# Turning the attention probabilities of a perceiver block: VectorE in blocks over all rows, ScalarE moving the pieces to their keys' rows

## Chip, cores and metric

The kernel runs on one core of one Trainium2 chip, in float32 throughout. The metric is the device time of one execution in microseconds (us). The time before is 783.33 us, the median of three runs (782.91 to 785.45).

## What is computed

There are B = 16 samples of S = 128 tokens with D = 512 features, and each sample has V = 2048 context rows of 512 features. The block is, cut to what matters:

```python
x = x + cross_attention(layernorm(x), ctx)      # softmax(x ctx^T) ctx, one head, 2048 keys
x = x + self_attention(layernorm(x))            # 16 heads of 32, rotary on half of each head, causal, 128 keys
x = x + ffn(layernorm(x))                       # h + two of eight low-rank experts, chosen by token 0 of the sample
```

The change touches the self attention only. For each of its 16 heads it has a 128 x 128 matrix of probabilities, queries on the rows. The product with the values needs it turned, keys on the rows. The mask is causal: with queries and keys cut into four groups of 32, query group i needs key groups j = 0 to i only, so ten of the sixteen 32 x 32 blocks of a head hold anything.

## The kernel before

**Layout.** A tile has 128 rows (partitions). `att` holds the probabilities of one sample as 128 queries x 16 heads x 128 keys. `pT` is one constant tile, 128 keys x 4 query groups x 16 heads x 32 queries, set to zero once at the start, so the six blocks per head above the diagonal are zero for good and only the ten others are written for each sample.

**The loop.** The main loop (line 849) has 14 passes, b = 0 to 13. It works on several samples at a time: in pass b the self attention is that of sample b, the cross attention's second half (`attend`) is that of sample a = b + 1, the cross attention's first half (`score`) is that of sample s = b + 2, and the expert stage is that of sample l = b - 1. The last two samples are finished after the loop in an order of their own, and they turn their probabilities on TensorE (`turn_heads`), which the change leaves alone.

**What sets the order.** Every engine and SP's DMA queue run their instructions in the order in which the program issues them; the wrapper `InOrder` keeps the scheduler from moving any. Inside an engine's queue an instruction that waits holds up all that follow it. All work goes through that wrapper, so the profile gives line 101 for nearly everything, and tiles are told apart by name.

**The stretch of a pass that the change is in**, in program order, with the engine of each step:

- `attend(a, 3)`, TensorE: the last matmuls into the two PSUM banks `av`; `whole(a)`: TensorE turns the partial sums into `den`.
- `attended(a)`, ScalarE: copies `moved` and the first half of `first` out of `av`.
- `turn_probs(b, 0)`, VectorE.
- `begin_join(a)`: VectorE adds into `moved`, then into `av`; then ScalarE copies the second half of `first`.
- `turn_probs(b, 1)`, VectorE.
- `joined(a)`, `portion(a)`, `x1_of(a)`, VectorE: two more adds into `av`, the softmax's divisor `rden`, the residual stream, and the moments of the second norm (`st`, `mv`). The second add overwrites what the copy of the second half of `first` reads, so it waits for that copy. GpSimd makes `rs` and `sh` from `mv`.
- `score(s, 0)`, TensorE, into a PSUM bank `psc`; `keep_score(s, 0)`: ScalarE copies it to `sc`.
- `turn_probs(b, 2)`, VectorE; `pair(l)`, ScalarE: copies `each`, which two gathering DMAs brought, to `paired`; `rows(2, a)`, ScalarE: the normed rows `h`, from `sh` and `rs`.
- `score(s, 1)`, TensorE; `keep_score(s, 1)`: ScalarE copies to `sc`, then VectorE takes the running maximum `mx` out of the same bank.
- `turn(2, a)`: VectorE turns `h` in 32 x 32 blocks into a tile `turn`, and SP's queue sends it through DRAM (`d`) back to the tile `hT`.
- `turn_probs(b, 3)`, VectorE.
- `rows(1, s+1)` on ScalarE and `turn(1, s+1)` as above, for a later sample.
- `score(s, 2)`, TensorE; `middle(l)`: TensorE `mid`, from `paired`, and ScalarE takes it out of PSUM; `keep_score(s, 2)`; `score(s, 3)`; `heads(b)`: TensorE multiplies `pT` with the values into `y`; `widen(l)`: `ffn`; `keep_heads(b)`: ScalarE copies `y` to `yT`; `keep_score(s, 3)`; `join(b)`: TensorE `o`, from `yT`.

**Banks and tiles.** The pool for `psc` has two banks, so `score(s, 2)` needs the bank of `score(s, 0)` empty again, and `score(s, 3)` needs that of `score(s, 1)`, copied by ScalarE and read by VectorE's maximum. Two engines that read one bank do so one after the other: the maximum waits for the copy. The tag `turn` has two buffers, used in turn.

**Turning before.** `turn_probs(b, i)` (line 556) takes query group i. For each key group j up to i one VectorE transpose reads rows 32i to 32i + 31 of `att`, all 16 heads, and writes the turned blocks to rows 32j to 32j + 31 of `pT`: 1, 2, 3 and 4 instructions of 32 x 512 in the four calls.

Of the kernel before, what the change touches and what calls it, by code (L numbers as in the profile page):

```python
# [11 lines left out]
F32 = mybir.dt.float32  # L12
# [7 lines left out]
P = 128  # L20
# [3 lines left out]
Q = P // 32  # L24
# [42 lines left out]
def perceiver_block(ctx: ExitStack, tc: tile.TileContext, io: dict, out: bass.AP):  # L67
# [4 lines left out]
    p2 = ctx.enter_context(tc.tile_pool(name="p2", bufs=2))  # L72
# [17 lines left out]
    pT = const.tile([P, Q, H, 32], F32, name="pT")  # L90
# [12 lines left out]
    pe, dve, act, pool, sp = map(InOrder, (nc.tensor, nc.vector, nc.scalar, nc.gpsimd, nc.sync))  # L103
# [17 lines left out]
    class Norm:  # L121
# [24 lines left out]
        def rows(self):  # L146
            of = p2 if self.tag == "h" else p1
            self.h = of.tile([P, D], F32, tag=self.tag, name=f"{self.tag}_{self.name}")[: self.n]
            to, of = self.h, self.src
            if self.by_act:  # L150
                act.activation(to, of, AF.Identity, bias=self.shift, scale=self.rstd)
                return self
            if self.mixed:
                to = to.rearrange("p (c a j) -> p c a j", c=KC, j=Q)
                of = of.rearrange("p (c j a) -> p c a j", c=KC, j=Q)
            dve.tensor_scalar(to, of, self.mv[:, 0:1], self.rstd, ALU.subtract, ALU.mult)
            return self
# [70 lines left out]
    def load_x(b):  # L228
        if b < B:
            xs[b] = p3.tile([P, D], F32, tag="x", name=f"x_{b}")  # L230
            load(xs[b], io["x"][b])

    def load_turned(b, v):
        if b < B:
            t = p4.tile([P, KC, 512], F32, tag="ctxT", name=f"ctxT_{b}_{v}")
            load(t, io["ctxT"][b, v])
            turned_cts[b, v] = t
# [13 lines left out]
    atts, ys, yTs, os_, routes, mids, ffns = ({} for _ in range(7))  # L251
# [4 lines left out]
    def turn(n, b):  # L256
        hTs[n, b] = norms[n, b].turned()
# [15 lines left out]
    def keep_score(b, v):  # L273
        if v == 0:
            scs[b] = p1.tile([P, VC, 4, S], F32, tag="blocks" if b == 1 else "sc", name=f"sc_{b}")
            mxs[b] = p1.tile([P, 4, S], F32, tag="mx", name=f"mx_{b}")
        sc, mx, ps = scs[b], mxs[b], psc.pop((b, v))
        act.copy(sc[:, v], ps)
        if 0 < v < VC - 1:
            dve.tensor_tensor(mx, ps, mx if v > 1 else sc[:, 0], ALU.max)  # L280
        if v == VC - 1:
            most = p1.tile([P, S], F32, tag="most", name=f"most_{b}")
            for to, in0, in1 in (
                (mx[:, 2:], ps[:, 2:], mx[:, 2:]), (ps[:, :2], ps[:, :2], mx[:, :2]),
                (mx[:, 3], ps[:, 1], mx[:, 3]), (ps[:, 0], ps[:, 0], mx[:, 2]), (most, ps[:, 0], mx[:, 3]),
            ):
                dve.tensor_tensor(to, in0, in1, ALU.max)
            mxs[b] = most
# [5 lines left out]
    def turn_max(b):  # L294
        trs[b] = bank(ps_acc, "acc", f"tr_m_{b}")
        transpose(trs[b][:, :S], mxs.pop(b), ident)

    def most(b):
        nm = p2.tile([P, 1], F32, tag="nm", name=f"nm_{b}")
        dve.tensor_reduce(nm, trs.pop(b)[:, :S], AX.X, ALU.max, negate=True)  # L300
        trs[b] = nm

    def spread(b):
        spreads[b] = bank(ps_acc, "acc", f"spread_{b}")
        transpose(spreads[b][:, :S], trs.pop(b).to_broadcast([P, P]), ident)

    def less(b, v):
        sc = scs[b]
        dve.tensor_tensor(
            sc[:, v], sc[:, v], spreads[b][:, None, :S].to_broadcast([P, 4, S]), ALU.add  # L310
        )

    def power(b, v):
        act.activation(scs[b][:, v], scs[b][:, v], AF.Exp)
# [145 lines left out]
    def project(b, n, ms=range(HC)):  # L460
        hT = hTs[2, b]
        if 0 in ms:
            projected[n, b] = bank(ps_acc, "acc", f"{n}_{b}")
        ps = projected[n, b]
        for m in ms:
            for c in range(KC):
                matmul(
                    ps[:, m * P : (m + 1) * P], w[n][:, c, m * P : (m + 1) * P], hT[:, :, c, :],
                    start=(c == 0), stop=(c == KC - 1),
                )  # L470

    def rotate(b, n, by=pool):
        ps = projected.pop((n, b))
        partner = p1.tile([P, HC, S], F32, tag=f"{n}P", name=f"{n}P_{b}")
        dve.stream_shuffle(partner.rearrange("p c t -> p (c t)"), ps, PARTNERS)
        ps = ps.rearrange("p (c t) -> p c t", c=HC)
        dve.tensor_tensor(
            ps, ps, cst[:, None, C_COS : C_COS + S].to_broadcast([P, HC, S]), ALU.mult
        )
        by.tensor_tensor(  # L480
            partner, partner, cst[:, None, C_SIN : C_SIN + S].to_broadcast([P, HC, S]), ALU.mult
        )
        partners[n, b] = ps, partner
# [6 lines left out]
    def order_tokens(b, copy=pool.tensor_copy):  # L490
        hTvs[b] = p1.tile([P, KC, S], F32, tag="hTv", name=f"hTv_{b}")
        copy(
            hTvs[b].rearrange("p c (i b) -> p c i b", i=Q),
            hTs[2, b].rearrange("p i c b -> p c i b"),
        )
# [57 lines left out]
            att[:, hs, :], att[:, hs, :], rsm[:, hs, None].to_broadcast([P, 4, S]), ALU.mult  # L553
        )

    def turn_probs(b, i):
        att = atts[b][0]
        for j in range(i + 1):
            dve.transpose(
                pT[j * 32 : (j + 1) * 32, i], att[i * 32 : (i + 1) * 32, :, j * 32 : (j + 1) * 32]  # L560
            )

    ACC, AV, SC = (ps_acc, "acc"), (ps_av, "av"), (ps_sc, "sc")

# [32 lines left out]
    def x2_of(b, later=False):  # L597
        x2s[b] = (p3 if b == B - 1 else p2).tile([P, D], F32, tag="x" if b == B - 1 else "x2", name=f"x2_{b}")
        dve.tensor_tensor(x2s[b], os_.pop(b), x1s[b], ALU.add)
        norms[3, b] = Norm(x2s[b], f"3_{b}", mixed=late(b), hT=(p2, "hT3"), by_act=b < B - 2).moments(later)  # L600
# [248 lines left out]
    for b in range(B - 2):  # L849
        l, a, s = b - 1, b + 1, b + 2  # L850
        if b:
            turn_max(a)
            most(a)
            x2_of(l)
        project(b, "q", [0, 1])
        if b:
            spread(a)
            for v in range(VC):
                less(a, v)
                power(a, v)  # L860
            load_x(s + 1)
            load_turned(s, 3)
        order_tokens(b, act.copy)
        if b:
            rows(3, l)
        project(b, "q", [2, 3])
        rotate(b, "q")
        project(b, "k")
        rotate(b, "k")
        if b:  # L870
            turn(3, l)
        project_v(b)
        keep_v(b)
        rotated(b, "q")
        rotated(b, "k")
        attend(a, 0, (0,))
        compare(b)
        attend(a, 1, (0,))
        if by_halves(a):
            token_halves(a)  # L880
        powers(b, 0)
        attend(a, 0, (1,))
        powers(b, 1)
        if b:
            shares(l)
        context_halves(a, 3)
        powers(b, 2)
        divided(b, 0)
        attend(a, 1, (1,))
        powers(b, 3)  # L890
        if b:
            logit(l)
        divided(b, 1)
        load_ctx(a + 1, 0)
        load_ctx(a + 1, 1)
        attend(a, 2)
        load_ctx(a + 1, 2)
        divided(b, 2)
        if b:
            sums(a)  # L900
        divided(b, 3, act)
        if b:
            choose(l)
            fetch(l)
            residual(l)
        if s + 1 < B:
            norm1(s + 1)
        attend(a, 3)
        load_ctx(a + 1, 3)
        whole(a)  # L910
        attended(a)
        turn_probs(b, 0)
        if b:
            gate(l)
        begin_join(a)
        turn_probs(b, 1)
        joined(a)
        portion(a)
        x1_of(a)
        score(s, 0)  # L920
        load_turned(s + 1, 0)
        keep_score(s, 0)
        turn_probs(b, 2)
        if b:
            pair(l)
        rows(2, a)
        score(s, 1)
        load_turned(s + 1, 1)
        keep_score(s, 1)
        turn(2, a)  # L930
        turn_probs(b, 3)
        if s + 1 < B:
            rows(1, s + 1)
            turn(1, s + 1)
        context_halves(a + 1, 0)
        context_halves(a + 1, 1)
        score(s, 2)
        load_turned(s + 1, 2)
        if b:
            middle(l)  # L940
        keep_score(s, 2)
        score(s, 3)
        heads(b)
        if b:
            widen(l)
            end(l)
        keep_heads(b)
        context_halves(a + 1, 2)
        keep_score(s, 3)
        join(b)  # L950
# [163 lines left out]
```

## Time and profile before

| | us |
|---|---|
| median of three runs | 783.33 (782.91 to 785.45) |
| the profiled execution: its time | 785.1 |
| its span, first to last instruction | 783.2 |
| TensorE busy | 767.5 (98%) |
| VectorE busy | 602.2 (77%) |
| GpSimd busy | 542.5 (69%) |
| ScalarE busy | 296.0 (38%) |
| 140 transposes of `att` into `pT`, VectorE | 98.2, 701 ns each |
| one pass of the loop (from `score(s, 0)` at 456.55 to the next at 502.25) | 45.7 |

The profile is of one execution, 1.9 us longer than its span and 1.8 us above the median of the runs. Busy time is an average over stages; what a change is worth is read from the waits of the stage that it is in. The granted TensorE clock is 0.994 over the span.

### The profile page before, as it was taken

What the parts mean: (1) busy time and instruction counts of PE and PEld (TensorE: products, weight loads), DVE (VectorE), ACT (ScalarE), POOL (GpSimd) and SP (SyncE); (2) the same over time, 40 slices, a digit from 0 to 9 for tenths busy, and PEclk for the clock granted to TensorE, in tenths of its full rate; (3) what the DMA queues carried; (4) which work ended last, traced back from release to release, by engine and by line L of the source; (5) the groups of instructions that cost most, each with busy time, mean ns of one, the idle gap of its engine ahead of it and who ended that gap; (6) DMA issues with size and microseconds to landing.
All of it is one profiled execution on the core that took longest, in us unless ns stands there. A gap on an engine that the chain in (4) does not pass through costs nothing.

```text
span 783.2 us, 16475 instructions
## 1 busy us (share of the span) xinstructions
PE 767.5 (98%) x6402; PEld 589.0 (75%) x6402; DVE 602.2 (77%) x1183; ACT 296.0 (38%) x893; POOL 542.5 (69%) x600
## 2 busy tenths in 40 slices
PE   8999999999999999999999999999999999999995
PEld 7946686879778687877868787786878788686653
DVE  2547568888797878879888887988888788877564
ACT  1222434244253424425343442534344243423160
POOL 2002477888879787887978888797888879735524
PEclk9999999999999999999999999999999999999997
DMA  9989865658586565957757595765659576531002
GB/s 371 408 315 405 301 246 199 231 217 310 191 299 251 194 226 204 331 191 273 279 181 243 198 334 190 274 239 218 239 204 334 189 262 249 197 128 41 28 1 94
DMA packets 57981, 181.75 MB, mean 232 GB/s; under 512 B 5504, under 2 KB 27392, under 8 KB 41520
## 3 DMA queue, kind: packets, MB, share of 16 engines
q1 hardware_dynamic: 53760, 168.38, 58.7%
q0 software_dynamic: 4000, 12.26, 4.5%
q8 instruction: 50, 0.82, 0.4%
q14 instruction: 27, 0.22, 0.1%
q10 hardware_dynamic: 144, 0.07, 0.0%
HBM read 165.48 MB, written 15.20 MB: 231 GB/s over the span
## 4 chain that ended last, share of the span: by engine, by line
PE 91%; DVE 3%; POOL 2%; DMA 2%; issue 1%; ACT 1%; POOLq 0%; ACTq 0%
PE psc L101 28%; PE av L101 25%; PE o L101 7%; PE q L101 7%; PE k L101 7%; PE v L101 6%; PE ffn L101 2%; PE pss L101 2%; PE y L101 2%; PE mid L101 2%; DMA each<-in_A_dram,g_blocks 1%; PE lg L101 1%; POOL more L101 0%; PE den L101 0%; PE tr_p L101 0%
## 5 line engine op out<-in xcount | busy, mean ns | idle before, releaser
L101 PE MATMUL psc<-hT,ctxT 128*128 128x128 f32 x2048 | 233.9, 275 | 1.4 <-DVE mx L101 0.8
L101 PEld LDWEIGHTS psc<-hT,ctxT 128*128 128x128 f32 x2048 | 231.9, 193 | 2.1 <-DVE mx L101 0.9
L101 PE MATMUL av<-ctx,sc 128*64 128x256 f32 (+1 forms) x512 | 153.4, 423 | 0.0
L101 POOL TENSOR_TENSOR more<-ctx 128x512 f32<-128x512 f32 x104 | 132.6, 1275 | 4.4
L101 ACT ACTIVATE att<-att,nmx 128x128 f32<-128x128 f32 x256 | 98.8, 387 | 56.6 <-DVE nmx L101 56.2
L101 PEld LDWEIGHTS av<-ctx,sc 128*64 128x64 f32 (+1 forms) x512 | 71.5, 147 | 54.7 <-issue 29.2
L101 DVE STREAM_TRANSPOSE pT<-att 32x512 f32<-32x512 f32 x140 | 98.2, 701 | 4.5 <-POOL att L101 1.4
L101 PE MATMUL av<-more,sc 128*64 128x256 f32 x416 | 85.1, 384 | 0.0
L101 POOL TENSOR_SCALAR rs<-mv 128x1 f32<-128x1 f32 x48 | 11.6, 241 | 96.9 <-DVE mv L101 94.7
L101 ACT ACTIVATE sc<-sc 128x512 f32<-128x512 f32 x64 | 38.5, 630 | 91.8 <-DVE sc L101 91.8
L101 POOL TENSOR_TENSOR ctx<-ctx 128x512 f32<-128x512 f32 x52 | 66.4, 1276 | 4.1
L101 POOL TENSOR_TENSOR more<-ctx,more 128x512 f32<-128x512 f32 x52 | 66.3, 1274 | 4.1
L101 PE MATMUL av<-ctx,blocks 128*64 128x256 f32 x416 | 63.2, 379 | 0.0
L101 PEld LDWEIGHTS q<-hT,w_q 128*128 128x128 f32 x512 | 59.5, 192 | 4.0 <-issue 3.9
L101 PE MATMUL av<-more,blocks 128*64 128x256 f32 x208 | 61.9, 380 | 0.0
L101 PE MATMUL q<-hT,w_q 128*128 128x128 f32 x512 | 61.4, 275 | 0.0
L101 PE MATMUL k<-hT,w_k 128*128 128x128 f32 x512 | 59.8, 275 | 0.0
L101 PE MATMUL o<-w_c,yT 128*128 128x512 f32 x128 | 58.4, 595 | 0.7 <-ACT yT L101 0.7
L101 PEld LDWEIGHTS k<-hT,w_k 128*128 128x128 f32 x512 | 58.5, 192 | 0.0
L101 POOL TENSOR_TENSOR att<-att,rsm 128x512 f32<-128x512 f32 x47 | 47.8, 1041 | 14.3 <-DVE rsm L101 14.3
L101 PE MATMUL v<-w_v,hTv 128*128 128x512 f32 x128 | 57.6, 593 | 0.0
L101 ACT COPY sc<-psc 128x512 f32<-128x512 f32 x64 | 37.1, 580 | 47.9 <-PE psc L101 47.9
(162 smaller groups left out, 1284.4 us busy)
## 6 DMA issues: line engine op xcount, KB each, us to landing
ctxT<-in_ctxT_dram SPq DMA_DIRECT2D x64, 1024.0 KB, 7.1
ctx<-in_ctx_dram SPq DMA_DIRECT2D x64, 1024.0 KB, 6.3
d<-turn SPq DMA_DIRECT2D x42, 256.0 KB, 2.7
hT<-d SPq DMA_DIRECT2D x42, 256.0 KB, 2.9
x<-in_x_dram SPq DMA_DIRECT2D x16, 256.0 KB, 6.1
out_dram<-x POOLq DMA_DIRECT2D x14, 256.0 KB, 6.7
down_q<-in_Wq_downT_dram SPq DMA_DIRECT2D x2, 1024.0 KB, 12.4
down_k<-in_Wk_downT_dram SPq DMA_DIRECT2D x2, 1024.0 KB, 10.5
```

The costliest lines, as they stand in the source:

```text
L101: return lambda *args, **kwargs: tc.keep_in_program_order(issue(*args, **kwargs))
```

## The change

`turn_probs` is now called for a group g of four heads instead of a group of queries. One VectorE transpose takes all 128 rows and the four heads, 128 x 512, turns every 32 x 32 block where it stands, and writes a tile `pturn` (tag `turn`, two buffers, shared with the turned norms). Each block is then right inside but still on its queries' rows. Ten ScalarE copies of 32 x 128 move the ten blocks of the causal half (four heads at a time) from rows 32i of `pturn` to rows 32j of `pT`. A pass thus issues four VectorE transposes in place of ten, and 40 ScalarE copies that were not there; in 14 passes 56 and 560. The first three calls stand where they stood; the fourth now comes before `turn(2, a)` and not behind it. The work of TensorE, GpSimd and the DMAs is the same, in the same order.

```diff
-    def turn_probs(b, i):
-        att = atts[b][0]
-        for j in range(i + 1):
-            dve.transpose(
-                pT[j * 32 : (j + 1) * 32, i], att[i * 32 : (i + 1) * 32, :, j * 32 : (j + 1) * 32]
-            )
+    def turn_probs(b, g):
+        t = p2.tile([P, Q, 4, 32], F32, tag="turn", name=f"pturn_{b}_{g}")
+        hs = slice(4 * g, 4 * g + 4)
+        dve.transpose(
+            t.rearrange("p j h b -> p h j b"),
+            atts[b][0][:, hs].rearrange("p h (j a) -> p h j a", j=Q),
+        )
+        for i in range(Q):
+            for j in range(i + 1):
+                act.copy(pT[j * 32 : (j + 1) * 32, i, hs, :], t[i * 32 : (i + 1) * 32, j])
...
         keep_score(s, 1)
+        turn_probs(b, 3)
         turn(2, a)
-        turn_probs(b, 3)
```

## Prediction

> **What bounds the kernel now.** I read the page's busy shares first, then who TensorE waited for, then one pass of the loop in order of time, engine by engine, and last the one pass in which TensorE was held up by the chain that the change lengthens.
>
> ```profile
> PE 767.5 (98%) x6402; PEld 589.0 (75%) x6402; DVE 602.2 (77%) x1183; ACT 296.0 (38%) x893; POOL 542.5 (69%) x600
> ...
> PE psc L101 <- DVE mx L101: 0.8, 1, 0.8
> ```
>
> TensorE is busy 98% and idle 15.7 us of 783.2 in all, mostly at both ends. Inside the loop it waits for VectorE once, 0.8 us. So VectorE's 602 us are no bound, and whatever delays TensorE inside a pass is paid in full. Now the pass that begins at 456.5, TensorE, ScalarE and VectorE in turn (start, length, instruction, idle before it):
>
> ```profile
> 456.55 10.88 PE L101 MATMUL psc<-hT,ctxT 128*128 128x128 f32 x96
> 467.27 1.06 PE L101 MATMUL mid<-hT,paired 128*128 128x128 f32 x8
> 468.16 3.74 PE L101 MATMUL psc<-hT,ctxT 128*128 128x128 f32 x32
> ...
> 456.50 0.58 ACT L101 COPY moved<-av 64x512 f32<-64x512 f32 x1 [1.41 <-PE av L101]
> 457.09 0.37 ACT L101 COPY first<-av 64x256 f32<-64x256 f32 x1
> 458.96 0.37 ACT L101 COPY first<-av 64x256 f32<-64x256 f32 x1 [1.50 <-DVE av L101]
> 460.38 0.58 ACT L101 COPY sc<-psc 128x512 f32<-128x512 f32 x1 [1.05 <-PE psc L101]
> 462.77 0.62 ACT L101 COPY paired<-each 128x512 f32<-128x512 f32 x1 [1.81 <-DMA each<-in_A_dram,g_blocks]
> 465.45 0.81 ACT L101 ACTIVATE h<-x,sh,rs 128x512 f32<-128x512 f32 x1 [2.07 <-POOL sh L101]
> 466.18 0.56 ACT L101 COPY sc<-psc 128x512 f32<-128x512 f32 x1
> ...
> 458.96 1.41 DVE L101 STREAM_TRANSPOSE pT<-att 32x512 f32<-32x512 f32 x2
> 460.40 0.71 DVE L101 TENSOR_TENSOR av<-av,moved 64x512 f32<-64x512 f32 x1
> ...
> 463.91 0.18 DVE L101 BATCH_NORM_AGGREGATE mv<-st 128x2 f32<-128x6 f32 x1
> 464.12 2.13 DVE L101 STREAM_TRANSPOSE pT<-att 32x512 f32<-32x512 f32 x3
> 466.77 0.69 DVE L101 TENSOR_TENSOR mx<-psc,sc 128x512 f32<-128x512 f32 x1 [0.52 <-ACT sc L101]
> ```
>
> ScalarE has gaps here of 1 to 2 us, and the change fills just these. The fourth score (psc at 468.16) needs the bank that `mx` leaves at 467.46: 0.7 us to spare. What the loss of that costs is shown by the pass in which the DMA of `each` came late:
>
> ```profile
> 282.65 0.62 ACT L101 COPY paired<-each 128x512 f32<-128x512 f32 x1 [5.56 <-DMA each<-in_A_dram,g_blocks]
> ...
> 284.48 0.69 DVE L101 TENSOR_TENSOR mx<-psc,sc 128x512 f32<-128x512 f32 x1 [2.10 <-ACT sc L101]
> ...
> 285.23 3.84 PE L101 MATMUL psc<-hT,ctxT 128*128 128x128 f32 x32 [0.75 <-DVE mx L101]
> ```
>
> `paired` late made `h`, `sc` and `mx` late; the score began 0.06 after `mx` (284.48 + 0.69 to 285.23), and that pass took 46.75 us (272.68 to 319.43) in place of 45.70. Nothing was won back.
>
> **What is taken away.** Per pass six of ten transposes: 701 ns each in `pT<-att`, and 704 ns for the same operation on 128 x 512 (`turn<-h`). 10 x 0.70 - 4 x 0.70 = 4.2 us of VectorE a pass, 59 us in 14. TensorE waited for none of them, so I count it at zero, save that the second call is 0.7 shorter ahead of the adds into `av`, which is in the sum below.
>
> **What one copy costs.** The trace has no copy of 32 x 128. From PSUM, 128x512 takes 580 ns and 64x256 takes 367: 213 ns for 256 elements, 0.83 each, fixed part 154. From SBUF, `hTv` takes 604 and `paired` 618 for 512: fixed part 178 to 192. So 128 elements take 0.285 to 0.30 us. What decides is whether neighbours overlap. Instructions over all rows do: `h` at 465.45 lasts 0.81, yet `sc` begins 0.73 later. That would make a pace of about 0.19. Those that change rows do not: `moved` (rows 0 to 63 into 64 to 127) lasts 0.58 and `first` begins 0.59 later, and VectorE's row-moving transposes run two in 1.41 and three in 2.13, 0.71 each for 0.70 of work. In the new copies each neighbour differs in its source or target rows. I take 0.30 and keep 0.19 as the other end.
>
> The Trainium skill, page "ScalarE: Activation LUTs", section "What ACT_TABLE_LOAD costs", gives an instruction with immediate operands 186 ns + 0.833 per element and an overlap of about 93 ns between neighbours. By it, as an estimate, the pace is 0.20 and the sum below 8 us in place of 35. The row that bears on this is `moved` and `first`, with no overlap; I follow the row.
>
> **The sum for one pass, with pace 0.30.** The first block transpose (VectorE, 455.20) is done long before. Its ten copies stand behind `first`: 457.47 to 460.47. The second `first` follows, 460.48 to 460.85, where it had ended at 459.33. The second add into `av`, which overwrites what `first` reads, starts at 460.88 and not 460.40. From there to the third transpose takes 3.72 as before (460.40 to 464.12): 464.60, done 465.30. Meanwhile ScalarE copies the second quarter, 460.85 to 463.85, and only then the first score's bank, to 464.44. The third score wants that bank at 463.70 (456.55 + two scores of 3.57), so TensorE stands 0.8. Third-quarter copies: 465.33 to 468.33. Then `paired` (0.52 to the next, as at 282.65), `h` (0.72 to the next; `sh` is ready by 466.0), `sc` from 469.58 to 470.14, `mx` to 470.86, fourth score at 470.92. It was 468.16: 2.76 lost, the 0.8 and a shorter wait at `mid` for `paired` inside it. With a pace c from about 0.2 up the loss is 20c - 3.25, since two batches of ten lie in the chain; where copies overlap and c is below that, only one does: 10c - 1.44, so 0.46 at 0.19.
>
> What is late next: the fourth quarter's copies run about 471.5 to 474.5; `y` wants them at 474.6. The later `h`, `mid`, `sc` and `yT` follow on ScalarE and come out level with `ffn` and `o`, nothing lost until c passes 0.31. `turn(2, a)` goes behind the fourth transpose: its transpose starts 4.0 later, at 471.4, and SP's two DMAs with it. Before, the second was issued at 470.74 and lands 2.9 later by the page's median, so about 477.7 now; `q` wants it at 477.35 + 2.76 = 480.1. Behind it on SP stand the other turned norm's two DMAs and three loads (`ctxT` twice, `x`), some 4 us later, for scores a pass away. The shared `turn` buffers bring no wait: each is asked for again two tiles later, when its copies or its DMA are over (third transpose 464.6, first copies 460.5).
>
> **All passes.** Thirteen passes have `moved` and `paired` (b = 1 to 13). Twelve lose 2.76; the one at 272 had lost 1.05 already and loses 1.7 more: 34.8. Pass b = 0 has neither, and ScalarE waits there 8.4 us before 94.60, so its copies are free. Against the profiled execution: 783.2 + 1.9 outside the span + 34.8 = 819.9. The median of the runs is 1.8 below that execution: 783.33 + 34.8 = 818.
>
> **The rivals.** A, end to end, as summed: 0.285 gives 2.45 a pass, 0.31 gives 3.1 with the first losses behind; 814 to 823, 808 to 828 with some error in the chain. Chance 0.69. B, the copies overlap as whole-row ones do: 0.17 to 0.20 gives 0.26 to 0.7 in twelve passes, 3 to 8 us, 786 to 792. For it: every whole-row pair on ScalarE; against: `moved` and `first`. Chance 0.18. C, on the other side, not slower: the copies fit the gaps. Its place is the bank that `mx` leaves, its point c = 0.144, where the loss is nil; up to 0.16 it is under 2.4 us. For it: ScalarE is busy only 38%, and it starts an accumulator read-out and the next exponential 0.09 apart; against: the fixed part of every copy. 783 to 785. D, faster: 4.2 us less on VectorE shortens a wait. Inside the loop the only wait to win is the 0.8 at 285, caused by a DMA, so it would lie within 0.3% (2.35 us, about what a measurement of this kernel can tell from no change); 0.03 for what I do not see. E, slower still: above 0.31 `y`, `ffn` and `o` wait too, by 0.34 some 3.9 a pass, 833. Chance 0.04.
>
> **How the numbers follow.** A is likeliest: 818. Range 787 to 828: A and nearly all of B; C, D, E and B's edge, about 0.16, are left out. Faster 0.03 (D), same 0.06 (C), slower 0.91 (A, B, E).
>
> **What would show it.** Right: groups `pturn<-att` x56 near 0.70 us and `pT<-pturn` x560 near 0.29, ten in 3.0; a wait of TensorE's `psc` for VectorE's `mx` in each pass, and one for ScalarE's `sc`; passes of 48.4 us. Ten copies in 1.9 and passes of 46.2 mean B; passes of 45.7 mean C and that the chain has slack that I missed. Wrong altogether: a pass lengthened by `hT` landing late or by `y` waiting for `pT` while the scores run on time.

## Result and the profile after

The changed kernel takes 821.92 us (median of four runs, 820.94 to 823.08) and the kernel before 784.39 us beside it: 1.0481 times as long, 95% interval 1.0457 to 1.0505. That is 37.5 us more, where 34.8 were forecast. The profiled execution is the longest of the four (823.08) and has a span of 821.3 us.

First the page of the changed kernel, busy time of each engine, then two of the groups (busy us, mean ns of one | idle time before them), then what TensorE waited for (us in total, times, longest):

```profile
span 821.3 us, 16949 instructions
...
PE 782.3 (95%) x6402; PEld 593.1 (72%) x6402; DVE 538.4 (66%) x1099; ACT 456.7 (56%) x1453; POOL 544.2 (66%) x600
```

```profile
L101 ACT COPY pT<-pturn 32x128 f32<-32x128 f32 x560 | 165.5, 295 | 32.4 <-DVE pturn L101 26.1
...
L101 DVE STREAM_TRANSPOSE pturn<-att 128x512 f32<-128x512 f32 x56 | 38.9, 696 | 0.4
```

```profile
PE psc L101 <- DVE mx L101: 9.8, 13, 0.8
PE psc L101 <- ACT sc L101: 9.0, 13, 0.7
PE mid L101 <- ACT paired L101: 5.0, 13, 0.4
```

VectorE is 64 us less busy and ScalarE 161 us more, and neither is near full. TensorE, with the same 6402 matmuls, now waits three times in each of 13 passes, for ScalarE twice and once for VectorE's maximum: 23.8 us. Its busy time rose by 14.8 us with no work added. Of these, 11.7 lie in the loop, where the modelled ends of pipelined matmuls stretch around each wait (a score after a wait reads 3.84 us, one without 3.74); the other 3.1 lie ahead of the loop and behind it. In the pass below, 1.83 us of waits and 0.93 more of busy time make up the 2.76 that it lost. A busy share of 95% thus hides part of the loss.

The pass that begins at 477.0, TensorE, ScalarE, VectorE in turn (start, length, instruction, idle before it):

```profile
477.01 7.31 PE L101 MATMUL psc<-hT,ctxT 128*128 128x128 f32 x64
485.02 3.84 PE L101 MATMUL psc<-hT,ctxT 128*128 128x128 f32 x32 [0.69 <-ACT sc L101]
489.24 1.16 PE L101 MATMUL mid<-hT,paired 128*128 128x128 f32 x8 [0.39 <-ACT paired L101]
491.15 3.84 PE L101 MATMUL psc<-hT,ctxT 128*128 128x128 f32 x32 [0.75 <-DVE mx L101]
...
477.55 0.37 ACT L101 COPY first<-av 64x256 f32<-64x256 f32 x1
477.82 3.06 ACT L101 COPY pT<-pturn 32x128 f32<-32x128 f32 x10
480.91 0.37 ACT L101 COPY first<-av 64x256 f32<-64x256 f32 x1
481.30 3.06 ACT L101 COPY pT<-pturn 32x128 f32<-32x128 f32 x10
484.38 0.59 ACT L101 COPY sc<-psc 128x512 f32<-128x512 f32 x1
485.49 3.06 ACT L101 COPY pT<-pturn 32x128 f32<-32x128 f32 x10 [0.53 <-DVE pturn L101]
488.57 0.62 ACT L101 COPY paired<-each 128x512 f32<-128x512 f32 x1
489.10 0.81 ACT L101 ACTIVATE h<-x,sh,rs 128x512 f32<-128x512 f32 x1
489.81 0.56 ACT L101 COPY sc<-psc 128x512 f32<-128x512 f32 x1
...
481.31 0.71 DVE L101 TENSOR_TENSOR av<-av,moved 64x512 f32<-64x512 f32 x1 [1.17 <-ACT first L101]
...
484.78 0.68 DVE L101 STREAM_TRANSPOSE pturn<-att 128x512 f32<-128x512 f32 x1
...
490.41 0.69 DVE L101 TENSOR_TENSOR mx<-psc,sc 128x512 f32<-128x512 f32 x1 [4.95 <-ACT sc L101]
```

Read it along the chain. The first ten copies keep the second `first` until 480.91, so VectorE's second add sits idle 1.17 us for it. The next ten keep the first bank's copy until 484.38, and the third score waits for that. The third ten begin when their transpose is done and push `paired`, `h`, `sc` and `mx` behind them, and the fourth score waits for `mx`. A pass takes 48.47 us (477.01 to 525.49) where it took 45.70.

### The profile page after: what moved, and what is told of

Read it like the earlier page. It is cut to its first block, busy times and chain, and to the rows that moved or that the text cites. A ratio compares the mean times of both kernels' runs of the same rounds, so it can differ in the third digit from the quotient of the medians.

```text
span 821.3 us, 16949 instructions
## 1 busy us (share of the span) xinstructions
PE 782.3 (95%) x6402; PEld 593.1 (72%) x6402; DVE 538.4 (66%) x1099; ACT 456.7 (56%) x1453; POOL 544.2 (66%) x600
## 4 chain that ended last, share of the span: by engine, by line
PE 72%; ACT 14%; DVE 10%; issue 2%; POOL 1%; DMA 0%; POOLq 0%; ACTq 0%
PE av L101 25%; PE psc L101 11%; ACT pT L101 9%; PE o L101 7%; PE q L101 7%; PE k L101 7%; PE v L101 6%; DVE av L101 2%; PE ffn L101 2%; PE pss L101 2%; PE y L101 2%; DVE x L101 1%; DVE st L101 1%; ACT first L101 1%; ACT h L101 1%
## 5 line engine op out<-in xcount | busy, mean ns | idle before, releaser
L101 PE MATMUL psc<-hT,ctxT 128*128 128x128 f32 x2048 | 239.9, 277 | 19.5 <-DVE mx L101 9.8
L101 PEld LDWEIGHTS psc<-hT,ctxT 128*128 128x128 f32 x2048 | 234.1, 193 | 25.1 <-DVE mx L101 12.3
L101 ACT COPY pT<-pturn 32x128 f32<-32x128 f32 x560 | 165.5, 295 | 32.4 <-DVE pturn L101 26.1
L101 DVE TENSOR_TENSOR mx<-psc,sc 128x512 f32<-128x512 f32 x16 | 11.1, 692 | 81.7 <-ACT sc L101 81.7
L101 DVE STREAM_TRANSPOSE turn<-h 128x512 f32<-128x512 f32 x42 | 29.2, 694 | 43.9 <-ACT h L101 43.9
## 6 DMA issues: line engine op xcount, KB each, us to landing
down_q<-in_Wq_downT_dram SPq DMA_DIRECT2D x2, 1024.0 KB, 12.3
```

What stands on the lines that cost most here:

```text
L101: return lambda *args, **kwargs: tc.keep_in_program_order(issue(*args, **kwargs))
```

## Experiments

The theory: the loss is what the copies add to one chain (two batches of ten, end to end at 0.307 us each), and they go end to end because each has other rows than its neighbour. The rivals: the loss goes by ScalarE's added load; it comes from the new order or from the shared `turn` buffers; or the copies are slow for another reason.

### What makes the copies go end to end

Ten copies stay at each place; only their rows differ, by group of heads.

```diff
-        for i in range(Q):
-            for j in range(i + 1):
-                act.copy(pT[j * 32 : (j + 1) * 32, i, hs, :], t[i * 32 : (i + 1) * 32, j])
+        rows = (((0, 0), (0, 0)), ((1, 1), (1, 1)), ((1, 2), (1, 2)), ((0, 0), (1, 1)))[g]
+        for k in range(10):
+            i, j = rows[k % 2]
+            act.copy(pT[j * 32 : (j + 1) * 32, k % 4, hs, :], t[i * 32 : (i + 1) * 32, k // 4])
```

> Ten copies of 32 x 128 stand where ten stood, but their rows differ by group of heads: group 0 all from rows 0-31 to rows 0-31, group 1 all from 32-63 to 32-63, group 2 all from 32-63 to 64-95, group 3 by turns 0-31 to 0-31 and 32-63 to 32-63. The blocks do not go to their keys' rows; that part is left out. With the changed kernel a batch of ten takes 3.06 us. Theory, neighbours overlap unless source or target rows change between them: groups 0, 1 and 2 about 2.0 us, group 3 about 3.1, and with the two batches of the chain at a pace of 0.20 the loss is 20 x 0.20 - 3.36 = 0.64 us a pass, about 793 us. Rival, copies of fewer than 128 rows never overlap: 3.1 us in all four groups and about 822 us. Rival, only a start at another row than 0 keeps them apart: group 0 2.0, the others 3.1. Rival, only a shift of rows does: group 2 3.1, the others 2.0.

The four batches of one pass, in the order of the groups, from ScalarE's timeline:

```profile
463.07 2.09 ACT L101 COPY pT<-pturn 32x128 f32<-32x128 f32 x10
...
465.58 2.09 ACT L101 COPY pT<-pturn 32x128 f32<-32x128 f32 x10
...
469.77 2.09 ACT L101 COPY pT<-pturn 32x128 f32<-32x128 f32 x10 [1.49 <-DVE pturn L101]
...
475.07 3.19 ACT L101 COPY pT<-pturn 32x128 f32<-32x128 f32 x10 [1.37 <-DVE pturn L101]
```

Three batches on constant rows take 2.09 us, at row 0, away from row 0 and with a shift of rows alike; the one that alternates takes 3.19. One copy lasts 290 to 300 ns in all of them, so it is the overlap that goes. The three rivals fall: it is neither the number of rows, nor the start, nor the shift, but the change of rows from one copy to the next. Nor is it a wait that the program puts between them: in the changed kernel's trace only the first copy of a batch carries one, and each of the nine others begins 0.303 to 0.311 us after the copy before it, those too of which only the source rows or only the target rows are new. The time is 795.84 us (one run), where about 793 was expected: the fourth score is 0.60 us late, near the 0.64 forecast for the pass, and behind the alternating fourth batch `ffn` and `o` come 0.26 later still.

Whole rows, in two forms. The first:

```diff
-                act.copy(pT[j * 32 : (j + 1) * 32, i, hs, :], t[i * 32 : (i + 1) * 32, j])
+                act.copy(pT[:, i, hs, :], t[:, j])
```

> Each of the 560 copies takes all 128 rows, 128 x 128, from and to the same rows, at the same place in the program; the move to the keys' rows is left out. Theory (the loss is the chain of two batches at the copies' pace, and whole-row copies overlap): ten in about 2.0 us, pace 0.19 to 0.20, loss 0.46 to 0.64 us in twelve passes, passes of 46.2 to 46.4 us, 790 to 793 us. Rival (it is the number of copies or their place in ScalarE's queue, or copies within one tile never overlap): ten in 3.0 us and 818 to 823 us.

```profile
471.53 2.87 ACT L101 COPY pT<-pturn 128x128 f32<-128x128 f32 x10
```

811.71 us: the theory missed, ten took 2.87 us and not 2.0. In this edit consecutive copies with the same i write the same place of `pT`, six of nine neighbours, which the edit had not meant. The trace parts the two kinds: in all 56 batches these six begin 0.323 to 0.332 us after the copy before, and each carries a wait for ScalarE's own semaphore; the three others begin 0.199 to 0.206 after it and carry none. The second form takes the overwriting away, with the four query groups by turns:

```diff
-        for i in range(Q):
-            for j in range(i + 1):
-                act.copy(pT[j * 32 : (j + 1) * 32, i, hs, :], t[i * 32 : (i + 1) * 32, j])
+        for k in range(10):
+            act.copy(pT[:, k % 4, hs, :], t[:, k // 4])
```

> As the run with 560 copies of 128 x 128, but no copy writes what the copy before it wrote: the four query groups of pT are taken by turns. The move to the keys' rows is left out. In the first such run six of nine neighbours wrote the same place and ten took 2.87 us, a pace of 0.286. Theory (same rows and different places: neighbours overlap; the 0.286 came from writing one place twice in a row): ten in 2.1 us, loss 0.64 to 1.0 us a pass as with the pieces of 32 rows on the same rows, 794 to 797 us. Rival (copies of all rows go end to end for another reason): 2.9 us and 810 to 813 us.

```profile
508.65 2.09 ACT L101 COPY pT<-pturn 128x128 f32<-128x128 f32 x10
```

2.09 us for ten and 793.61 us in all; each pass takes 46.28 us, 0.57 over the kernel before, where 0.64 was worked out for a pace of 0.20 ahead of the run on constant rows. So two things kept neighbours apart here: other rows, with no wait between the copies, and a wait for the copy that is overwritten. A wait alone need not do it: from the fifth copy on these, too, wait for ScalarE's own semaphore, since the place that they write was last written four copies earlier, and they keep the pace of 0.20. Whole rows have no advantage over 32 rows.

### Copies out, transposes in

```diff
-        for i in range(Q):
-            for j in range(i + 1):
-                act.copy(pT[j * 32 : (j + 1) * 32, i, hs, :], t[i * 32 : (i + 1) * 32, j])
```

> The four block transposes stay and all copies are left out, so pT stays zero. Theory (VectorE's 4.2 us a pass are worth nothing, the new place of the fourth transpose and the shared buffers cost nothing): same as before, 783 to 786 us, passes of 45.7 us. Rival, the new order or the shared turn buffers carry part of the loss: over 790. Rival, less work on VectorE is worth something by itself: under 781.

785.28 us, 1.0001 times the kernel before (0.9975 to 1.0027), passes of 45.71 us. The whole loss is the copies'. Taking 64 us from VectorE is worth nothing that can be measured, and the new order costs nothing by itself. The shared buffers have no copies to wait for in this run; in the changed kernel, where they have, VectorE stood idle 0.4 us in all ahead of the 56 transposes (the line in the first section), so they cost nothing there either.

### One batch out at a time

In each of four kernels one group's ten copies are left out and the other thirty stay:

```diff
+        if g == 0:      # 1, 2, 3 in the other three
+            return
         for i in range(Q):
```

> The ten copies of the first group of heads are left out (their probabilities stay zero). Theory of the chain, with the copies' measured pace of 0.307: the second half of first is copied at once, the second add into av starts at 460.40 less the 0.7 us of the shorter transpose, the third transpose is done at 464.11, then ten copies (3.07), paired, h, sc and mx: fourth score at 469.8 for 468.16, a loss of 1.65 us a pass in place of 2.8, about 806 us. Rival (each batch costs its share of the added load): a quarter less loss, 2.1 a pass, about 812.

> The ten copies of the second group of heads are left out (their probabilities stay zero). Theory of the chain: this batch runs while VectorE makes the moments, beside the chain, so the loss stays at 2.8 us a pass and the time at 820 to 823 us; only its place changes, the third score no longer waits for ScalarE's sc and the whole loss stands at mid and the fourth score. Rival (load): 2.1 a pass, about 812.

> The ten copies of the third group of heads are left out (their probabilities stay zero). Theory of the chain: paired, h, sc and mx are no longer held up beyond the first 0.8 us, h waits for sh at 465.9, the fourth score is in time after the third: loss 0.8 us a pass, all at the third score for sc, about 794 us. Rival (load): 2.1 a pass, about 812.

> The ten copies of the fourth group of heads are left out (their probabilities stay zero). Theory of the chain: they lie behind mx and are done by the time y wants them, so nothing changes: 2.8 us a pass, 820 to 823 us. Rival (load): 2.1 a pass, about 812. Rival (y, ffn or o already wait for what follows these copies): 0.1 to 0.3 us a pass less, 818 to 820.

| left out | time, us | one pass, us | less than 48.47 | forecast by the chain | by the load |
|---|---|---|---|---|---|
| first batch | 805.08 | 47.33 | 1.14 | 1.15 | 0.7 |
| second | 830.97 | 48.47, in five passes 50 | 0, or 1.5 more | 0 | 0.7 |
| third | 798.20 | 46.67 | 1.80 | 2.0 | 0.7 |
| fourth | 822.35 | 48.33 | 0.14 | 0 (0.1 to 0.3 if `y`, `ffn` or `o` wait) | 0.7 |

The four are not alike, so the load theory falls. The first and the third batch are the two of the chain. The second runs while VectorE makes the moments and can go without gain; then the third score no longer waits, but the whole loss stands further on. The fourth is nearly hidden: without it `o` begins 0.03 earlier after the score and takes 3.60 us in place of 3.70, together the 0.14 but for rounding.

The second row missed: 831 where 820 to 823 was expected. Here are the two waits of TensorE in each of two neighbouring passes, then the two stretches that follow the first wait of the earlier pass, and then the two passes whole (stretch, its length, busy time and number of each engine, and near the end the granted clock, DMA share, GB/s):

```profile
445.26 1.16 PE L101 MATMUL mid<-hT,paired 128*128 128x128 f32 x8 [1.35 <-ACT paired L101]
447.17 5.47 PE L101 MATMUL psc<-hT,ctxT 128*128 128x128 f32 x32 [0.76 <-DVE mx L101]
...
495.23 1.16 PE L101 MATMUL mid<-hT,paired 128*128 128x128 f32 x8 [1.35 <-ACT paired L101]
497.14 3.84 PE L101 MATMUL psc<-hT,ctxT 128*128 128x128 f32 x32 [0.75 <-DVE mx L101]
```

```profile
445.20:449.00 3.80, 2.99 (x18) 2.80 (x19) 1.90 (x3) 2.38 (x7) 3.64 (x4) 0.82 0.02 4
449.00:453.00 4.00, 4.00 (x40) 3.88 (x43) 1.28 (x2) 3.31 (x9) 3.62 (x3) 0.75 0.39 131
```

```profile
432.86:482.83 49.97, 47.87 (x401) 37.67 (x400) 34.06 (x69) 27.05 (x86) 37.35 (x41) 0.97 0.62 220
482.83:531.30 48.47, 46.37 (x401) 35.93 (x399) 34.17 (x70) 26.96 (x86) 38.99 (x42) 1.00 0.62 228
```

In seven of its twelve full passes the length is as forecast or within 0.5 of it. In five it is 1.5 to 1.8 us more, and the granted TensorE clock is down: 0.97 over such a pass, and in this one 0.82 from the end of the first wait to 449.0 and 0.75 in the next 4 us; its fourth score takes 5.47 us in place of 3.84. The waits are the same in both passes, so they alone do not decide whether the clock falls. With all forty copies the clock stays at 1.00 in every pass of the profiled execution. Two more runs:

> The kernel without the second group's ten copies again (their probabilities stay zero), timed beside the kernel before. Theory (its whole wait stands in one stretch ahead of mid and the fourth score, and the granted TensorE clock falls after that in some passes): 826 to 834 us in every run, passes of 48.5 us where the clock stays at 1.0 and about 50.0 where it falls. Rival (a chance event of that one execution): 819 to 823 us.

827.30 us (826.03 to 830.00), 1.0548 times the kernel before (1.0509 to 1.0587), again five long passes of 49.95 to 49.97: not chance. Leaving out 140 copies makes this kernel slower than the changed one (1.0457 to 1.0505). Its passes with the clock at 1.00 are as long as the changed kernel's, 48.47 us; what it loses in the loop beyond that it loses in the five long ones. What sets its waits apart is that they are longer and nearer to each other: 2.10 us within 3.3, where the changed kernel has 1.83 us within 6.8. The next run has the waiting in one piece:

```diff
+        if g == 1:
+            return
...
-        turn_probs(b, 2)
         if b:
             pair(l)
+        turn_probs(b, 2)
```

> Without the second group's copies, and with paired ahead of the third group's copies, so that mid is on time and all the waiting stands at the fourth score. The third group's probabilities are there, the second's stay zero. Chain: third transpose done 465.3, ten copies 3.07, h 0.72, sc 0.56, mx 0.72: fourth score at 470.5 for 468.16, 2.3 us a pass in one piece. If the clock falls by the length of the waits near to one another (2.1 us of idle within 4 us), passes of 48.0 and some of 49.5, 815 to 828 us. If it needs two waits around a short burst of mid: passes of 48.0 only, 814 to 816 us.

818.22 us. With `mid` on time there is one wait of 1.83 us; passes are 47.94, 2.24 us over the kernel before (2.3 expected). One of the twelve full passes is 49.44, and the clock also falls in the shorter pass behind them, b = 13 (43.70 us, granted clock 0.96). So the clock came down in two of 13 passes, against five of 13 with 2.10 us in two pieces and none of 13 with the changed kernel's 1.83 us in three. These are one or two executions of each kernel; whether the length of the idle time or its spacing decides was not settled.

### The place of the fourth call

```diff
-        turn_probs(b, 3)
         turn(2, a)
+        turn_probs(b, 3)
```

> The changed kernel with the fourth call behind turn(2, a), where it stood before the change. Theory (the fourth batch and its place are off the chain): 820 to 824 us, passes of 48.5 us, the fourth batch 0.6 us later, so y, ffn or o may wait 0.1 to 0.6 us more, up to 830. Rival (the new place costs, since the turned norm is sent 0.7 us later): under 818 us.

830.34 us, passes of 49.06, just past the far end of what was expected (830). The fourth transpose is 0.6 later, and now `y` waits for its copies:

```profile
500.01 1.60 PE L101 MATMUL y<-pT,vv 128*32 128x128 f32 x32
```

`y` takes 1.60 us in place of 1.08. Moving the call forward, as the change does, therefore saved 0.6 us a pass. That the turned norm goes later costs nothing that shows: TensorE's waits for `hT` are the two of 0.7 us that the kernel before has too.

### The same move in ten copies a pass, put into the gaps

All 16 heads go into one tile, so that ten copies of 32 x 512 do what forty of 32 x 128 did, and they stand behind the bank copies that TensorE waits for.

```diff
+    def turn_probs(b, gs):
+        if 0 in gs:
+            pturns[b] = p1.tile([P, Q, H, 32], F32, tag="blocks", name=f"pturn_{b}")
+        for g in gs:
...
+    blocks = [(i, j) for i in range(Q) for j in range(i + 1)]
+    def move_probs(b, which):
+        for i, j in blocks[which]:
+            act.copy(pT[j * 32 : (j + 1) * 32, i], pturns[b][i * 32 : (i + 1) * 32, j])
...
+        turn_probs(b, (0,))              # behind gate(l), ahead of begin_join(a)
+        turn_probs(b, (1, 2, 3))         # where the second call stood
+        move_probs(b, slice(0, 6))       # behind keep_score(s, 0)
+        move_probs(b, slice(6, 10))      # behind keep_score(s, 1)
```

> The four block transposes write one tile for all 16 heads (in the tag blocks, free at that time), one after the end of av and three where the second call stood; then ten copies of 32 x 512, six behind the first score's bank copy and four behind the second's. ScalarE's copies cost 0.604 + 0.01 each, 6.1 us a pass in place of 12.3, no batch stands ahead of a bank copy that TensorE waits for, and h is 0.7 us later because of the third transpose. Theory (the loss is where the copies stand in the chain): fourth score at most 0.1 us late, passes of 45.7 to 45.8 us, 783 to 787 us. Rival (the loss goes by ScalarE's added load): half of the 38 us, about 803.

```profile
460.29 3.76 ACT L101 COPY pT<-pturn 32x512 f32<-32x512 f32 x6
...
465.92 0.56 ACT L101 COPY sc<-psc 128x512 f32<-128x512 f32 x1
466.51 2.50 ACT L101 COPY pT<-pturn 32x512 f32<-32x512 f32 x4
...
467.56 3.74 PE L101 MATMUL psc<-hT,ctxT 128*128 128x128 f32 x32
```

785.19 us, 1.0013 times the kernel before (0.9996 to 1.003), passes of 45.71, the fourth score in time. ScalarE carries 86 us of copies here and TensorE notices none of them. So the four block transposes and a move on ScalarE need not cost anything. The run changes two things at once, the copies' place and their time (6.3 us a pass where the forty took 12.3), and does not say whether the place alone would do; that ScalarE's load does not set the loss was shown by leaving out one batch at a time. The version does not beat the kernel before either: TensorE is the bound, and in the kernel before it had no wait in this stretch but the one of 0.75 us in the pass at 272.

## Why the prediction was right, step by step

- **The bound and the worth of VectorE's time.** Zero was forecast for 59 us less of VectorE; without the copies the time is that of the kernel before, 1.0001 (0.9975 to 1.0027).
- **The price.** 0.285 to 0.30 was forecast for one copy and 0.30 taken as the pace: one lasts 0.295, ten take 3.06, a pace of 0.307. The choice between 0.30 and 0.19 rested on the rows `moved` and `first` of the profile before, and the reason given there, a change of rows, is the one that the runs show. Rival B's pace would have held on constant rows: ten in 2.09 us, and 793.61 us for the kernel that has such copies throughout. The Trainium skill, page "ScalarE: Activation LUTs", section "What ACT_TABLE_LOAD costs", gives, as an estimate, 293 ns for 128 elements (186 ns + 0.833 per element) and, less about 93 of overlap, a pace of 0.20: on constant rows the runs agree, where the rows change they do not (0.307).
- **The chain.** Shifted to this pass (20.46 later), the forecast put the second `first` at 480.94, the second add at 481.34, the third transpose at 485.06, its copies at 485.79, `sc` at 490.04 and the fourth score at 491.38. Measured: 480.91, 481.31, 484.78, 485.49, 489.81 and 491.15. One term was mis-sized by more than 0.1: from the second add to the third transpose VectorE took 3.47 us, not 3.72. The fourth score is 2.53 late and not 2.76.
- **What is late next** was forecast as level, and it was not quite: after its wait the score takes 0.10 longer, `o` starts 0.03 later beyond that (5.77 after the score, where it was 5.64) and itself takes 0.10 longer (3.70 for 3.60). The three make up for the 0.23, and the pass is 2.76 longer, as forecast (48.47 for 45.71). That the two errors cancel is luck: the sum for the pass is closer than its terms.
- **The sum.** From the first `den` of the loop to the one behind the loop it is 669.26 us (92.67 to 761.93) and was 634.46 (90.72 to 725.18): 34.8, as forecast. The other 3.3 us of the span's 38.1 lie ahead of the first `den` (1.95) and behind the last (1.35), where the change has no part. The 1.95 is within what executions differ by there: the kernel without the second batch had that `den` at 94.04 us in one execution and at 90.86 in another. Behind the loop the granted clock was 0.88 where it was 0.93; why is open. The kernel before itself spreads from 782.63 to 788.91 over 19 runs on one chip.
- **What the prediction did not see.** It priced the new place of the fourth call only as a cost to the turned norm. The place is a gain: without it a pass would be 0.6 us longer.
- **Rivals C, D, E.** C and D fell with the copies' pace and with the run without copies. E's threshold of 0.31 was set slightly too high; the beginning of it shows at 0.307: 0.13 a pass by `o`; without the fourth batch `o` is back to what it was before, and the pass is 0.14 shorter.

## What to carry to other kernels

An engine that is 38% busy can still not take work at any place: look at which of its results the bound engine waits for in that stretch, and put what is added behind those, in as few and as long instructions as the tiles allow. Price small instructions by pairs of neighbours of the same kind in the trace, not by one instruction's length: whether neighbours overlap was here the difference between some 8 us (793.61 for 785.25 beside it) and 37. Leave one batch out at a time to find which are on the chain; equal shares of load need not cost equal shares of time, and one batch here cost nothing or less.

## What the hardware showed that was not expected

- **Overlap on ScalarE.** Copies of 128 elements a row last 0.293 to 0.297 us on average. On the same rows and into different places ten take 2.09 us, 0.20 each. Where source or target rows change between neighbours, ten take 3.06 (with no wait between them) to 3.19. Where a copy waits for the one that it overwrites just before it, it begins 0.323 to 0.332 after it.
- **The clock can fall at short waits.** With TensorE idle 1.35 and then 0.75 us within 3.3 us, the granted clock fell in five of 13 passes in each of two executions, in one of them to 0.82 and 0.75 in the two stretches of some 4 us behind the first wait, at a loss of 1.5 us or a little more each; with one wait of 1.83 us it fell in two of 13; with 0.69, 0.39 and 0.75, the first 3.8 us ahead of the others, in none. The Trainium skill, page "TensorE: Matmul & The Clock Gate", Part 1, puts the fall after an idle window of about 3.4 us that runs freely. That some passes are hit and others not agrees with a window that runs freely, but the measured idle stretches are shorter than it.
